# Output projection beside the attention: from full 128x128 matmuls in one stretch to 64x32 tiles in two parts

## The chip, the cores and the metric

The kernel runs on one core of a Trainium2 chip, as one launch. The metric is the device time of that launch in microseconds (us), the median of several runs.

## The reference

Two graph layers work on `x` of 8 batches x 2048 nodes x 256 features, in fp32, with one 2048 x 2048 0/1 adjacency for all batches. The first layer is multi-head attention (4 heads of 64) in which each query row takes a softmax over every chunk of 256 keys by itself, and the chunks' results are added up. The second is a graph attention of rank one. Cut to what matters here:

```python
h = jnp.maximum(_layernorm(x), 0.0)
q, k, v = (h @ Wq.T + bq), (h @ Wk.T + bk), (h @ Wv.T + bv)      # split into 4 heads of 64
scores = jnp.einsum('bhnd,bhjcd->bhnjc', q, kc) / 8.0              # 8 chunks j of 256 keys
scores = jnp.where(mask == 0, -10.0, jnp.clip(scores, -10.0, 10.0))
ctx = jnp.einsum('bhnjc,bhjcd->bhnd', jax.nn.softmax(scores, axis=-1), vc)
out = ctx @ Wo.T + bo + h                                          # the output projection
x = x + _layernorm(out) * gamma + beta
...                                                                # layer 1: rank-one graph attention
```

The change concerns `ctx @ Wo.T`, a product of 2048 x 256 by 256 x 256 for each batch.

## The kernel before, in words

The order of the instructions on every engine is written out by hand, and each engine runs its own queue in that order; waits between engines are put in by the framework from the data that they share.

A batch's attention has 32 steps: 4 blocks `nb` of 512 queries, times 8 chunks `j` of 256 keys. The loop in `gnn_two_layers` runs over `f`, and each `f` has two halves, `Attention.begin(f)` and `Attention.end(f)`. Several steps are in flight: `f-1` makes logits, `f-2` and `f-3` are multiplied with the values.

All attention matmuls are small tiles of TensorE: 64 rows (half of the contraction rows) by 32 columns, so eight of them fit at once, four in each half of the rows. "Half 0" below is rows 0 to 63, "half 1" is rows 64 to 127. The kernel always issues four matmuls for one half and then four for the other, so that both halves work side by side. An fp32 matmul appears in the trace as two weight loads and two matmul records.

- `logits(n, o, kt)` (L401): the logits of head `ORDER[o]`, into a PSUM tile `ps_s`, of which there are two. Heads 0 and 2 of the order use half 1, heads 1 and 3 use half 0.
- `clip(n, o)` (L441): VectorE reads the finished `ps_s` tile, clips and masks it into `e`, and so frees that tile.
- `values(n, half, c, kt)` (L417): products of `e` with the values, into two `ps_n` tiles. `sums(n, half)` (L429): the softmax denominators, into a `ps_t` tile, of which there are two; `invert` (L461) on ScalarE reads that. `scale` (L471) multiplies the two, and `gather` (L476) adds the result into `ctxT` by an accumulating DMA.
- `fence(before, after)` (L373): an empty instruction on SyncE that waits for some matmuls and lets others go. It stands where both halves of the rows write one bank of PSUM one after the other.

`begin(f)` issues on TensorE: `values(f-3)`, then pieces marked `pe`, then `logits(f-1, 1)` and `logits(f-1, 2)` in turn. `end(f)` issues: `values(f-2)`, `logits(f-1, 3, 0)`, `sums(f-2, 1)`, `logits(f-1, 3, 1)`, `logits(f, 0, 0)`, pieces, `sums(f-2, 0)`, `logits(f, 0, 1)`. On VectorE `begin` has clip 0 and the two scales, and `end` has `first` pieces, clip 1, clip 2, other pieces, clip 3.

The work that follows the attention of a block of queries is cut into pieces (`Between`) and laid beside the attention of the next block: `beside()` gives each piece a slot, counted in halves of `f`. Even slots fall into a `begin`, odd ones into an `end`; pieces without a mark in an even slot run in the `end` that follows, after clip 2. Three of the four blocks of a batch are treated so, 24 in all. The fourth block of each batch has its projection after the attention, by the unchanged `output` and `take`.

In the kernel before, slot 8 has `output(0)` and `output(1)` (L600): 8 matmuls of 128 x 128 x 256, 16 records, into both `ps_t` tiles. Slot 9 has `take` (L609), in which VectorE adds the residual `hn0` to 512 columns of PSUM at a time, and the layernorm's `stats` (L260, L261); the first two stand ahead of clip 1.

Of the kernel before, what the change touches and what calls it, by code (L numbers as in the profile page):

```python
# [8 lines left out]
F32 = mybir.dt.float32  # L9
# [4 lines left out]
ALU = mybir.AluOpType  # L14
# [3 lines left out]
P = 128  # L18
# [10 lines left out]
def gnn_two_layers(  # L29
# [18 lines left out]
    nc = tc.nc  # L48
    B, N, F = x.shape
    FC = F // P  # L50
    DH = F // HEADS
    Q = P // 4
# [3 lines left out]
    TB = NB // P  # L56
    NNB = N // NB
# [16 lines left out]
    def ps_t():  # L74
        return ps.tile([P, 512], F32, tag="t", name="ps_t")
# [4 lines left out]
    def ps_m():  # L80
        if turn_about[0]:
            turn_about[1] += 1
            if turn_about[1] % 2:
                return ps_n()
        return ps_t()
# [8 lines left out]
    work = ctx.enter_context(tc.tile_pool(name="work", bufs=2, reuse_waits="tile"))  # L94
# [14 lines left out]
    woT = const.tile([P, FC, F], F32, name="woT")  # L109
# [47 lines left out]
    def first(piece):  # L157

        piece.kind = "first"
        return piece  # L160

    def pe(piece):

        piece.kind = "pe"
        return piece


# [27 lines left out]
    def load_rows(t, half):  # L195
        rows = xpool.tile([P, HALF], I32, tag="x", name="rows", bufs=NNB)
        nc.sync.dma_start(rows, adj[t * P:(t + 1) * P, half * HALF:(half + 1) * HALF])
        return rows
# [32 lines left out]
    def adjacency(parts):  # L231


        def load(i):
            rows[i] = load_rows(*parts[i])

        def find(i):
            found[i] = missing_of(rows.pop(i), *parts[i])

        def turn(i):  # L240
            found[i] = turn_missing(found[i])

        def keep(i):
            keep_bounds(found.pop(i), *parts[i])

        finds = [9, 11, 15, 17, 21, 23, 29, 31]
        turns = [12, 12, 18, 18, 26, 26, 32, 32]
        todo = {}
        for i, (f, t) in enumerate(zip(finds, turns)):
            todo.setdefault(f - 6, []).append(lambda i=i: load(i))  # L250
            todo.setdefault(f, []).append(lambda i=i: find(i))
            todo.setdefault(t, []).append(pe(lambda i=i: turn(i)))
            todo.setdefault(t + 1, []).append(first(lambda i=i: keep(i)))
        return todo
# [18 lines left out]
    def norm_tiles(tag, bufs):  # L273
        mv = small.tile([P, TB, 2], F32, tag="mv", name="mv")
        rn = small.tile([P, 2, TB], F32, tag=tag, name=tag, bufs=bufs)
        return mv, rn
# [19 lines left out]
    class Projection:  # L296
# [32 lines left out]
        def take(self, nb, c):  # L329
            if c == 0:  # L330
                nc.vector.tensor_copy(self.hT[nb][:, 0, :], self.pt.pop(c))
            else:
                nc.scalar.activation(self.hT[nb][:, 1, :], self.pt.pop(c), AF.Copy)
# [37 lines left out]
    def fence(before, after):  # L371

        nop = nc.sync.nop()  # L373
        for x in before:
            tc.add_manual_dep(nop.ins, x.ins.name, SYNC, reason="both write one bank of PSUM")
        for x in after:
            tc.add_manual_dep(x.ins, nop.ins.name, SYNC, reason="both write one bank of PSUM")


    class Attention:  # L380
# [159 lines left out]
        def end(self, f, pieces=()):  # L540
            self.run(pieces, "first")
            if self.has(f - 1):
                self.clip(f - 1, 1)
                self.clip(f - 1, 2)
            self.run(self.rest, None)
            if self.has(f - 1):
                self.exponentials(f - 1, 1)
                self.exponentials(f - 1, 2)
            if self.has(f - 2):
                made = {}  # L550
                for kt in range(KT):
                    for half, c in ((0, 1), (1, 0)):
                        made.setdefault(c, []).extend(self.values(f - 2, half, c, kt))
                for c in range(2):
                    self.before[f - 2, c] = made[c]
            if self.has(f - 1):
                self.logits(f - 1, 3, 0)
            if self.has(f - 2):
                sums = self.sums(f - 2, 1)
            if self.has(f - 1):  # L560
                self.logits(f - 1, 3, 1)
            if self.has(f):
                self.logits(f, 0, 0)
            self.run(pieces, None)
            self.run(pieces, "pe")
            if self.has(f - 2):
                fence(sums, self.sums(f - 2, 0))
            if self.has(f):
                self.logits(f, 0, 1)
            if self.has(f - 1):  # L570
                self.clip(f - 1, 3)
                self.add(f - 1, 0)
# [8 lines left out]
    class Between:  # L581
# [12 lines left out]
        def output(self, t2):  # L594
            ctxT = self.attention.ctxT[self.nb]
            pp = self.pp[t2] = ps_m()
            for i in range(2):
                t = 2 * t2 + i
                for c in range(FC):
                    nc.tensor.matmul(  # L600
                        pp[:, i * F:(i + 1) * F], ctxT[:, c, t * P:(t + 1) * P], woT[:, c, :],
                        start=c == 0, stop=c == FC - 1,
                    )

        def take(self, t2):
            if t2 == 0:
# [90 lines left out]
        def beside(self):  # L697

            todo = {
                -3: [self.load],  # L700
                3: [lambda: self.residual(0)],
                4: [lambda: self.residual(1)],
                5: [lambda: self.bias(0)],
                6: [lambda: self.bias(1)],
                8: [pe(lambda: self.output(0)), pe(lambda: self.output(1)), lambda: self.beta(0)],
                9: [
                    first(lambda: self.take(0)), first(lambda: self.stats([0])),
                    first(lambda: self.take(1)), first(lambda: self.stats([1])), lambda: self.stats([2]),
                ],
                10: [lambda: self.stats([3]), lambda: self.beta(1)],  # L710
                12: [self.power],
                13: [self.shift],
                14: [lambda: self.scaled(range(TB))],
                15: [lambda: self.gamma(0)],
                16: [lambda: self.gamma(1)],
                18: [lambda: self.add(0)],
                20: [lambda: self.add(1)],
            }

            def at(n, *pieces):  # L720
                todo.setdefault(n, []).extend(pieces)

            if self.nb == NNB - 2:
                return todo
            for t, n in enumerate((20, 22, 26, 28)):
                at(n, lambda t=t: self.stats1([t]))
            at(29, self.power1)
            at(30, self.shift1)
            if self.nb == 1:
                at(31, lambda: self.norm1(0))  # L730
                at(32, lambda: self.norm1(1))
            return todo
# [115 lines left out]
    rows = {i: load_rows(*nearest[i]) for i in range(4)}  # L848
# [69 lines left out]
    def layer1_vector(i):  # L918
# [11 lines left out]
        1: [lambda: raws.update(o=load_output_weight(wo)), layer1_weight],  # L930
        2: [lambda: store_bounds(0), lambda: store_bounds(1)],
        5: [pe(lambda: turn_weight(raws["o"], woT))],
        6: [lambda: layer1_vector(0)],
        7: [lambda: layer1_vector(1)],
# [8 lines left out]
    for b in range(B):  # L943
# [3 lines left out]
        zero, low, mid, last = blocks  # L947
# [260 lines left out]
```

The softmax here doesn't subtract the row's maximum and nothing guards it: scores larger than these inputs give would overflow.

## Time and profile before

| what | value |
|---|---|
| device time, median of 3 runs | 3649.71 us (3645.97 to 3652.3) |
| profiled span | 3645.0 us |
| TensorE busy | 3607.6 us, 99% of the span |
| VectorE, ScalarE, GpSimd busy | 71%, 54%, 49% |
| granted TensorE clock | 0.999 |
| L600, the output projection | 512 matmul records, of which 448 into `ps_t` and 64 into `ps_n` |
| L609, its take by VectorE | 64 instructions, median 692 ns |
| L441, the clips | 1024 instructions, 1220 ns each |

"Busy" counts the time in which at least one record of the engine is open. Eight tiles of TensorE can be open at once, so the durations of the attention matmuls (590 ns each) don't add up to time; how fast the groups of four follow each other does. The view called windows gives the busy time of each engine in stretches of the span, and the timeline lists the groups of instructions by their start.

### The profile page before, as it was taken

The page shows a single profiled execution, that of the slowest core. Times are in us where ns is not written, and L with a number is a line of the kernel's source. Part 1 is how long each engine was busy: PE and PEld are TensorE (multiplying, and loading weights), DVE is VectorE, ACT ScalarE, POOL GpSimd, SP SyncE. Part 2 cuts the span into 40 slices and gives each one's busy share as a digit, 9 for nine tenths or more (in the row PEclk, how much of TensorE's full clock was granted, in tenths as well). Part 3 has the DMA queues.
Part 4 walks back from the last instruction along what each step waited for, and adds up shares of the span by engine and source line. Part 5 has one row for each costly group of instructions (what it writes and reads, how often), then busy time and mean ns, then how long its engine had stood idle before and what let it go on. Part 6 is the DMA issues. An engine that isn't in the chain of part 4 may idle for free.

```text
span 3645.0 us, 99457 instructions
## 1 busy us (share of the span) xinstructions
PE 3607.6 (99%) x43952; PEld 2210.2 (61%) x43952; DVE 2582.9 (71%) x3915; ACT 1958.0 (54%) x2975; POOL 1788.8 (49%) x1142
## 2 busy tenths in 40 slices
PE   7999999999999999999999999999999999999999
PEld 4444785547754577455874558645586455865568
DVE  5887577866777666776667866678576785767866
ACT  5677416774167732677326762367713667147650
POOL 0678016870178702786027850378403774048731
PEclk9999999999999999999999999999999999999999
DMA  7444113341133411343113431134312332124321
GB/s 224 115 104 97 44 53 83 83 106 29 64 81 82 103 34 59 83 95 88 47 47 83 101 77 47 53 83 95 77 52 59 86 87 64 47 53 89 77 53 35
DMA packets 133281, 276.93 MB, mean 76 GB/s; under 512 B 26608, under 2 KB 91888, under 8 KB 124656
## 3 DMA queue, kind: packets, MB, share of 16 engines
q0 software_dynamic: 32256, 117.45, 17.7%
q1 hardware_dynamic: 83952, 151.01, 12.1%
q8 instruction: 344, 5.64, 0.7%
q10 hardware_dynamic: 16640, 2.10, 0.4%
q14 instruction: 89, 0.73, 0.1%
HBM read 132.12 MB, written 20.97 MB: 42 GB/s over the span
## 4 chain that ended last, share of the span: by engine, by line
PE 95%; DMA 2%; ACT 1%; DVE 1%; POOL 0%; issue 0%; POOLq 0%; ACTq 0%; SPq 0%; DVEq 0%
PE ps_n L417 24%; PE ps_s L401 24%; PE ps_s L800 12%; PE ps_t L429 6%; PE ps_n L800 6%; PE ps_t L800 6%; PE ps_t L600 3%; PE ps_t L345 2%; PE ps_n L345 2%; PE ps_s L345 2%; PE ps_n L674 2%; PE ps_t L674 2%; PE ps_t L359 1%; PE ps_n L359 1%; DMA ctxT<-prod 1%; PE ps_t L292 1%
## 5 line engine op out<-in xcount | busy, mean ns | idle before, releaser
L456 POOL TENSOR_TENSOR both<-e 128x1024 f32<-128x1024 f32 x512 | 1218.2, 2409 | 660.3 <-PE ps_s L401 258.9
L441 DVE SCALAR_TENSOR_TENSOR e<-ps_s,bound 128x1024 f32<-128x1024 f32 x1024 | 1220.1, 1220 | 377.3 <-PE ps_s L401 375.3
L401 PE MATMUL ps_s<-q,k 64*32 64x512 f32 x16384 | 1362.6, 590 | 2.1 <-DVE e L441 2.1
L450 ACT ACTIVATE e<-e 128x1024 f32<-128x1024 f32 x1024 | 1049.2, 1049 | 549.8 <-DVE e L441 530.4
L417 PE MATMUL ps_n<-e,v 64*32 64x512 f32 x16384 | 1164.3, 590 | 6.3 <-DVE prod L471 4.0
L417 PEld LDWEIGHTS ps_n<-e,v 64*32 64x32 f32 x16384 | 446.2, 107 | 504.4 <-issue 393.3
L401 PEld LDWEIGHTS ps_s<-q,k 64*32 64x32 f32 x16384 | 435.7, 106 | 461.0 <-issue 332.4
L817 POOL TENSOR_TENSOR x<-x,r 128x256 f32<-128x256 f32 x128 | 98.5, 770 | 1137.5 <-DVE rz L810 1006.3
L429 PE MATMUL ps_t<-both,ones 64*32 64x512 f32 x4096 | 538.0, 591 | 0.5
L800 PE MATMUL ps_s<-g,w 128*128 128x257 f32 x2048 | 448.7, 380 | 0.0
L471 DVE TENSOR_TENSOR prod<-ps_n,rz 128x512 f32<-128x512 f32 x448 | 288.7, 686 | 192.4 <-PE ps_n L417 86.1
L800 PEld LDWEIGHTS ps_s<-g,w 128*128 128x128 f32 x2048 | 388.3, 190 | 54.9
L783 DVE SCALAR_TENSOR_TENSOR w<-bound,w 128x1024 f32<-128x1024 int8 x256 | 313.7, 1225 | 8.7
L800 PE MATMUL ps_n<-g,w 128*128 128x257 f32 x1024 | 292.6, 382 | 0.0
L800 PE MATMUL ps_t<-g,w 128*128 128x257 f32 x1024 | 290.1, 380 | 0.0
L777 DVE TENSOR_SCALAR w<-src,cd 128x512 f32<-128x512 f32 x512 | 265.2, 560 | 9.8 <-ACT src L771 9.4
L461 ACT ACTIVATE rz<-ps_t 128x512 f32<-128x512 f32 x256 | 152.6, 596 | 177.4 <-PE ps_t L429 102.6
L476 POOL DMA_DIRECT2D ctxT<-prod x224 | 194.5, 868 | 55.0 <-DVE prod L471 52.4
L800 PEld LDWEIGHTS ps_n<-g,w 128*128 128x128 f32 x1024 | 192.6, 190 | 43.4 <-issue 17.6
L800 PEld LDWEIGHTS ps_t<-g,w 128*128 128x128 f32 x1024 | 194.0, 189 | 28.1
L429 PEld LDWEIGHTS ps_t<-both,ones 64*32 64x32 f32 x4096 | 121.9, 106 | 93.0 <-SPq L373 52.3
L462 ACT ACTIVATE rz<-rz 128x512 f32<-128x512 f32 x256 | 161.4, 630 | 8.1
(127 smaller groups left out, 2849.4 us busy)
## 6 DMA issues: line engine op xcount, KB each, us to landing
ctxT<-prod POOLq DMA_DIRECT2D x224, 512.0 KB, 4.9
bound<-bound_d SPq DMA_DIRECT2D x62, 1024.0 KB, 5.3
xp<-in_x_dram SPq DMA_DIRECT2D x60, 512.0 KB, 4.7
rows<-in_adj_dram SPq DMA_DIRECT2D x32, 512.0 KB, 5.5
x<-in_x_dram SPq DMA_DIRECT2D x32, 512.0 KB, 5.3
out_dram<-x SPq DMA_DIRECT2D x31, 512.0 KB, 2.9
bound_d<-bound_part ACTq DMA_DIRECT2D x16, 128.0 KB, 4.5
bound_d<-bound SPq DMA_DIRECT2D x2, 1024.0 KB, 6.4
```

What stands on the lines that cost most here:

```text
L345: nc.tensor.matmul(pp, w[:, di, do * P:(do + 1) * P], self.hT[nb][:, di, :], start=di == 0, stop=di == FC - 1,)
L401: nc.tensor.matmul(self.s[n, o][c * Q:(c + 1) * Q, kt, :], self.k[p][rows, at:at + Q], self.q[p][rows, nb * NB:(nb + 1) * NB], start=True, ...
L417: made.append(nc.tensor.matmul(self.num[n, c][h * Q:(h + 1) * Q, :], self.v[rows, j * KT + kt, at:at + Q], self.e[n, p][rows, i * KT + kt, :],
L429: nc.tensor.matmul(self.total[n][h * Q:(h + 1) * Q, :], ones[rows, :], self.both[n, h // 2][rows, h % 2, :], start=half == 1, stop=half == 0,)
L441: nc.vector.scalar_tensor_tensor(self.e[n, p][:, i * KT:(i + 1) * KT, :], self.s.pop((n, o)), -CLIP * SC, bounds[nb][:, j * KT:(j + 1) * K ...
L450: nc.scalar.activation(e, e, AF.Exp, scale=1.0 / SC)
L456: nc.gpsimd.tensor_tensor(self.both[n, p], e[:, 0], e[:, 1], op=ALU.add)
L471: nc.vector.tensor_tensor(dst[:, c, :], self.num.pop((n, c)), self.rz[n], op=ALU.mult)
L476: nc.gpsimd.dma_start(self.ctxT[nb], self.prod.pop(n), accum_op=ALU.add)
L777: nc.vector.tensor_scalar(w[:, i, :], self.src[nb], self.cd[:, 0, j:j + 1], self.cd[:, 1, j:j + 1], op0=ALU.mult, op1=ALU.max,)
L783: nc.vector.scalar_tensor_tensor(two, bounds1[nb][:, j - 1:j + 1, :], 0.0, two, op0=ALU.is_gt, op1=ALU.mult)
L800: nc.tensor.matmul(accs[t][:, 0:F + 1], w[:, i, t * P:(t + 1) * P], g[:, j, :], start=j == 0, stop=j == NT - 1,)
```

## The change

The projection beside the attention is made in the same 64x32 tiles as the attention, so that TensorE need not change its tiling for it. Every matmul of 128 x 128 x 256 becomes eight of 64 x 32 x 256. Half 0 and half 1 of the contraction rows both contribute to every output and may not write one bank of PSUM together, so the work is cut into two parts ("turns"): in turn 0 half 0 writes `pp[0]` and half 1 writes `pp[1]`, in turn 1 they change places. Turn 0 stands where the projection stood, ahead of the two slots of logits of `begin`; turn 1 follows them, at the head of the TensorE work of `end`; and a fence between the turns sees that a bank's first writers are done. Slot 9's `take` becomes four additions of 256 columns (`take_tiles`), which stand between clip 1 and clip 2 on VectorE, and the `stats` move to later places.

```diff
         def end(self, f, pieces=()):
...
                 self.clip(f - 1, 1)
+            self.run(pieces, "pe1")
+            self.run(pieces, "mid")
+            if self.has(f - 1):
                 self.clip(f - 1, 2)
...
+        def output_tiled(self, turn):
+            ctxT = self.attention.ctxT[self.nb]
+            if turn == 0:
+                self.pp = {t2: ps_t() for t2 in range(2)}
+                self.made = {}
+            made = {}
+            for i in range(2):
+                for c in range(FC):
+                    for half in range(2):
+                        t2 = half ^ turn
+                        rows = slice(half * DH, (half + 1) * DH)
+                        for h in range(4):
+                            at = (2 * t2 + i) * P + h * Q
+                            job = nc.tensor.matmul(
+                                self.pp[t2][h * Q:(h + 1) * Q, i * F:(i + 1) * F], ctxT[rows, c, at:at + Q],
+                                woT[rows, c, :], start=turn == 0 and i == 0 and c == 0,
+                                stop=turn == 1 and i == 1 and c == FC - 1,
+                            )
+                            made.setdefault(t2, []).append(job)
+            for t2 in range(2) if turn else ():
+                fence(self.made[t2], made[t2])
+            self.made = made
+
+        def take_tiles(self, i):
...
+            for t2 in range(2):
+                nc.vector.tensor_tensor(
+                    self.o4[:, 2 * t2 + i, :], self.pp[t2][:, i * F:(i + 1) * F], self.hn0[t2][:, i, :], op=ALU.add
+                )
...
-                8: [pe(lambda: self.output(0)), pe(lambda: self.output(1)), lambda: self.beta(0)],
+                8: [pe(lambda: self.output_tiled(0)), lambda: self.stats([0]), lambda: self.beta(0)],
                 9: [
-                    first(lambda: self.take(0)), first(lambda: self.stats([0])),
-                    first(lambda: self.take(1)), first(lambda: self.stats([1])), lambda: self.stats([2]),
+                    pe1(lambda: self.output_tiled(1)), mid_clips(lambda: self.take_tiles(0)),
+                    mid_clips(lambda: self.take_tiles(1)), lambda: self.stats([1]),
                 ],
-                10: [lambda: self.stats([3]), lambda: self.beta(1)],
+                10: [lambda: self.stats([2]), lambda: self.beta(1)],
+                11: [lambda: self.stats([3])],
```

## The prediction

> **What bounds the kernel now.** I read the page's busy shares and its chain of waits first, then the windows over four steps of `f`, then the timeline around one projection.
>
> ```profile
> PE 3607.6 (99%) x43952; PEld 2210.2 (61%) x43952; DVE 2582.9 (71%) x3915; ACT 1958.0 (54%) x2975; POOL 1788.8 (49%) x1142
> ...
> PE 95%; DMA 2%; ACT 1%; DVE 1%; POOL 0%; issue 0%; POOLq 0%; ACTq 0%; SPq 0%; DVEq 0%
> ```
>
> TensorE is busy throughout and is 95% of the chain, so time is won only by taking TensorE time away, and lost by making TensorE wait. The windows are, in order: a plain step, the step with a projection, and the two steps after it.
>
> ```profile
> 597.11:604.83 7.73, 7.73 (x152) 4.02 (x144) 6.06 (x6) 5.24 (x7) 5.53 (x4) 1.00 0.37 70
> 624.57:636.62 12.04, 12.04 (x172) 6.25 (x164) 9.07 (x15) 5.24 (x6) 6.82 (x4) 1.00 0.24 46
> 636.62:644.34 7.72, 7.72 (x152) 3.88 (x144) 6.52 (x9) 5.24 (x6) 6.87 (x4) 1.00 0.19 37
> 644.34:652.15 7.81, 7.81 (x148) 3.63 (x140) 5.96 (x7) 5.83 (x9) 5.78 (x4) 1.00 0.65 141
> ```
>
> A plain step is 7.72 us. It has 144 small matmul records, 18 groups of four for each half of the rows, so a group takes 0.429 us per half: TensorE runs without a gap although VectorE is busy for about 6 of the 7.7 us. The step with the projection is 4.32 us longer, and a busy share of 100% hides that not all of this is work.
>
> ```profile
> 624.57 0.61 PE L417 MATMUL ps_n<-e,v 64*32 64x512 f32 x4
> 624.68 0.61 PE L401 MATMUL ps_s<-q,k 64*32 64x512 f32 x4
> 625.00 2.00 PE L417 MATMUL ps_n<-e,v 64*32 64x512 f32 x28
> 626.93 3.72 PE L600 MATMUL ps_t<-woT,ctxT 128*128 128x256 f32 x16
> 630.58 1.95 PE L401 MATMUL ps_s<-q,k 64*32 64x512 f32 x32
> 632.32 1.92 PE L417 MATMUL ps_n<-e,v 64*32 64x512 f32 x32
> ...
> 629.03 0.69 DVE L609 TENSOR_TENSOR o<-ps_t,hn 128x512 f32<-128x512 f32 x1 [1.15 <-PE ps_t L600]
> 630.76 0.69 DVE L609 TENSOR_TENSOR o<-ps_t,hn 128x512 f32<-128x512 f32 x1 [0.35 <-PE ps_t L600]
> 632.57 2.36 DVE L441 SCALAR_TENSOR_TENSOR e<-ps_s,bound 128x1024 f32<-128x1024 f32 x2 [0.57 <-PE ps_s L401]
> ```
>
> The reader is to see that at 624.57 half 0 already starts the values while half 1, at 624.68, still has a last group of logits: half 1 is 0.54 us behind. Half 0 has done its four groups by 624.57 + 1.71 = 626.29, half 1 by 626.82; L600 starts at 626.93. So half 1 loses 0.11 us and half 0 0.64. After 3.65 us both halves start level at 630.58.
>
> **What the Trainium skill says.** "TensorEngine Tiling (Array Packing)", Key Properties: a change of the tiling mode drains TensorE. The trace agrees: 0.11 us for the later half, 0.64 for the earlier. "TensorE: Matmul & The Clock Gate", Part 3, The mechanism: matmuls are in strict program order at start and end. The trace differs: half 0's values start ahead of half 1's logits, which precede them in the program. The measurement decides, and the slip between the halves matters below. "PSUM — Partial Sum Buffer", on bank collisions: different row tiles may not access one bank together; software must synchronize. That is what the fence is for; no run here shows a collision. Price: "TensorEngine Tiling", Instruction Overhead, puts some 60 cycles on each matmul, an estimate of 25 ns at the 2.4 GHz that the TensorE page gives.
>
> **The change part by part.**
>
> *Removed.* L600 in 24 places; 16 records at 0.216 us are 3.45 us of work each. What a place costs in all: after the first and second block of a batch the halves are 0.54 us apart again two steps later (half 0 at 652.15 as at 624.57), because in the window from 644.34 half 1 waits for the second scale, which waits for a DMA. So three steps, 12.04 + 7.72 + 7.81 = 27.57, less 3 x 7.72 = 23.16, give 4.41 us. After the third block no such step comes before the batch's next full-size matmuls, which align the halves anyway; there half 1, which finishes last, lost 4.32 - 0.43 (its lag falls from 0.54 to 0.11) = 3.89 us.
>
> *Added on TensorE.* 64 matmuls of 256 columns are 128 records, 16 groups of four per half. At half of 0.429 us a group this is 16 x 0.215 = 3.44 us, the same work as before; the trace shows no small matmul of 256 columns. Bounds: 3.44 if the array sets the pace; 6.86 if a 256-column record costs as much as one of 512 (weight load included). I take 3.44: eight records now have 215 ns, 27 ns each, over the 25 ns that the price gives at full clock, and a small weight load of 107 ns fits into 215. No tiling changes and no alignment: 0.97 us saved at the first two blocks, 0.45 at the third.
>
> *The fence.* Half 0's turn 1 waits for half 1's turn 0. Two slots of logits, 4 groups or 1.71 us, lie between; half 0 is 0.54 ahead, so about 1.0 us is left after the last record's 0.16 us tail. SyncE's fence at L373 shows no wait of TensorE itself, only of weight loads (52.3 us in 248). Behind it are the values; cost nothing. The `ps_t` tile that half 1 needs at once was freed by the Ln of `invert`, which ends at 625.51 against 626.82; nothing either.
>
> *VectorE, the new wait.* `take_tiles` waits for the whole of turn 1 (only its first instruction waits for TensorE), and clip 2 is queued behind it. Who waits for clip 2: `logits(f, 0)` in half 1, which needs its `ps_s` tile. Costs: two scales of 0.68 take 1.29 together, so 512 columns are 0.61 apart; clips of 1.22 take 2.36, so 1024 are 1.14 apart; hence 256 columns are 0.61 - 0.27 = 0.34. From the moment T at which half 1 ends turn 1: 0.28 (tail 0.16 and 0.11 to start, as from L600's end at 630.65 to 630.76), takes 4 x 0.34 = 1.36, clip 2 1.14 and 0.08 to its end, 0.08 to TensorE: T + 2.94. Half 1 meanwhile has values 1.71 and sums 0.86: T + 2.57. It waits 0.37. Then VectorE has stats 0 and 1, 2 x 0.64 (L260 to L261 0.46, L261 0.18), clip 3 1.14, clip 0 1.22, then 0.08: from T + 2.78 to T + 6.50. Half 1 needs clip 0 for `logits(f, 2)` after four groups of logits and four of values, 2.94 + 3.43 = T + 6.37. It waits 0.13 more. Together 0.5, with two reloads of weights 0.52 us per block. In the kernel before, takes and two stats lay under L600 and the logits, ending at 632.00 before clip 1 could start at 632.57: hidden. Now the takes are not. Clip 1 itself comes earlier and waits for nothing new; stats 2 and 3 in the next step fit its free VectorE time (6.5 of 7.7 busy). SyncE, GpSimd and ScalarE keep their order.
>
> *Sum.* Some 15 blocks win 0.97 - 0.52 = 0.45, some 9 (the third of each batch, and the first of batch 0, which starts with the halves nearly level) lose 0.52 - 0.45 = 0.07: 6.75 - 0.63 = 6.1 us. 3649.7 - 6.1 = 3643.6 us. With the waits at 0.35 to 0.75 the gain is 10 to 1 us.
>
> **The rivals.**
> A, the wait on clip 2 is hidden: if the takes start by parts, or half 1's lag absorbs them, 0.1 us per block is left: 15 x 0.87 + 9 x 0.35 = 16, 3634 us. For it: plain steps absorb all of VectorE's lateness. Against: takes wait for half 1's end, so a lag of half 1 shifts both alike.
> B, small 256-column matmuls do not reach the array's pace. At worst 3.42 us x 24 = 82 - 6: 3726 us; half of it, 3685. For it: twice the records per time, never shown. Against: after stalls, groups of eight start 7 ns apart.
> C, the waits chain: VectorE's or the fence's lateness costs 1.1 us per block, as when stats push clip 3 and the next scales: 9 x 0.65 + 15 x 0.13 = 8 slower, 3657 us. For it: VectorE's queue from the takes to clip 0 is 6.2 us without a gap. Against: everything after it has slack of half a microsecond or more.
>
> **How the numbers follow.** Forecast 0.48, A 0.28, B 0.10, C 0.14. 0.2% is 7.3 us. The forecast's 10 to 1 us of gain gives faster 0.14, same 0.33, slower 0.01; A faster 0.26, same 0.02; B slower 0.10; C same 0.06, slower 0.08: faster 0.40, same 0.41, slower 0.19. The range leaves out B and the far ends of A and C: 3632 to 3662.
>
> **What would show it.** Right: small records of L633 in groups of four 0.215 us apart per half, no gap ahead of them, the halves still 0.5 us apart after them; the four takes in a row 0.3 us after turn 1's end; a gap of about 0.4 us in half 1 before `logits(f, 0)`, released by the clip, and a step with projection of about 11.7 us. Wrong: groups further apart than 0.215 (B), TensorE waiting on SyncE at L633 or for scales (C), or no gap at `logits(f, 0)` (A).

## The result and the profile after

The changed kernel takes 3634.21 us (median of 4 runs, 3632.24 to 3639.86) against 3648.95 for the kernel before in the same comparison: a ratio of 0.9962, interval 0.9945 to 0.9979, so 7.7 to 20 us less. The profiled span is 3630.0 us against 3645.0. The prediction had 3643.6 us, a gain of 6.1.

The busy times and the shares of the chain of waits, on the page of the changed kernel:

```profile
PE 3594.1 (99%) x46640; PEld 2205.1 (61%) x46640; DVE 2577.4 (71%) x3963; ACT 1961.8 (54%) x2975; POOL 1791.5 (49%) x1142
...
PE 97%; DMA 1%; ACT 1%; DVE 1%; issue 0%; POOL 0%; ACTq 0%; POOLq 0%; SPq 0%; DVEq 0%
```

TensorE is the bound as before, with 2688 more records (24 blocks of 128 in place of 16). Its busy time fell by 13.5 us although the arithmetic is the same: "busy" counts a time as work even when one half of the rows stands still in it. Where that was is seen in the same block as in the prediction. First the windows: the step with the projection and the two steps after it (columns: length, then PE, PEld, DVE, ACT, POOL, clock, DMA share, GB/s).

```profile
621.44:632.69 11.25, 11.25 (x280) 6.71 (x272) 7.75 (x14) 5.04 (x6) 6.86 (x4) 1.00 0.26 50
632.69:640.71 8.02, 8.02 (x156) 3.16 (x148) 7.76 (x12) 5.45 (x7) 6.85 (x4) 1.00 0.23 44
640.71:648.43 7.72, 7.72 (x152) 4.01 (x144) 5.86 (x7) 5.85 (x9) 5.78 (x4) 1.00 0.56 129
```

The step is 11.25 us, where it was 12.04. The next one is 0.30 longer than a plain step, and the third is a plain 7.72, where it was 7.81. In sum, 11.25 + 8.02 - 2 x 7.72 - 3.44 of work leaves 0.39 us lost per block; before it was 0.97, the third step included.

The timeline of TensorE through the projection (start, length, instructions; L425 is the values, L409 the logits, L437 the sums, L633 the projection):

```profile
621.44 0.61 PE L425 MATMUL ps_n<-e,v 64*32 64x512 f32 x4
621.54 0.61 PE L409 MATMUL ps_s<-q,k 64*32 64x512 f32 x4
...
623.16 0.40 PE L633 MATMUL ps_t<-woT,ctxT 64*32 64x256 f32 x4
623.26 0.61 PE L425 MATMUL ps_n<-e,v 64*32 64x512 f32 x4
623.37 1.79 PE L633 MATMUL ps_t<-woT,ctxT 64*32 64x256 f32 x52
624.88 0.62 PE L409 MATMUL ps_s<-q,k 64*32 64x512 f32 x4
624.98 0.61 PE L633 MATMUL ps_t<-woT,ctxT 64*32 64x256 f32 x8
...
626.60 0.41 PE L633 MATMUL ps_t<-woT,ctxT 64*32 64x256 f32 x4
626.70 0.61 PE L409 MATMUL ps_s<-q,k 64*32 64x512 f32 x4
626.82 1.79 PE L633 MATMUL ps_t<-woT,ctxT 64*32 64x256 f32 x52
628.33 0.63 PE L425 MATMUL ps_n<-e,v 64*32 64x512 f32 x4
628.43 0.61 PE L633 MATMUL ps_t<-woT,ctxT 64*32 64x256 f32 x8
...
631.00 0.61 PE L437 MATMUL ps_t<-both,ones 64*32 64x512 f32 x4
631.33 1.08 PE L409 MATMUL ps_s<-q,k 64*32 64x512 f32 x8
```

Half 0 starts turn 0 at 623.16 while half 1 still has a group of values, and is done with the 8 groups of this turn at 624.88, when its logits start: 1.72 us, 0.215 per group, the work and nothing more. Half 1 is still 0.54 behind after both turns: half 0 starts its values at 628.33, and half 1 has two more groups of the projection from 628.43 on, until about 628.865. Turn 1 starts at 626.60, right behind half 0's logits, so the fence holds nobody. The price appears at the end: half 1's last group of sums starts at 631.00, so it could go on at 631.43, but its logits do not start then. The weight loads show it, and VectorE's timeline shows why:

```profile
631.78 0.13 PEld L409 LDWEIGHTS ps_s<-q,k 64*32 64x32 f32 x5 [0.73 <-DVE e L449]
```

```profile
626.85 1.23 DVE L449 SCALAR_TENSOR_TENSOR e<-ps_s,bound 128x1024 f32<-128x1024 f32 x1 [2.10 <-PE ps_s L409]
629.18 1.42 DVE L648 TENSOR_TENSOR o<-ps_t,hn 128x256 f32<-128x256 f32 x4 [1.10 <-PE ps_t L633]
630.51 1.22 DVE L449 SCALAR_TENSOR_TENSOR e<-ps_s,bound 128x1024 f32<-128x1024 f32 x1
631.64 0.42 DVE L268 BATCH_NORM_STATS2 stats<-o 128x6 f32<-128x256 f32 x1
...
632.19 0.40 DVE L268 BATCH_NORM_STATS2 stats<-o 128x6 f32<-128x256 f32 x1
...
632.72 2.32 DVE L449 SCALAR_TENSOR_TENSOR e<-ps_s,bound 128x1024 f32<-128x1024 f32 x2
```

VectorE is idle from 628.08 to 629.18, waiting for turn 1. Then it makes the four takes (L648), and clip 2 (630.51 to 631.73) behind them frees the tile that half 1 needs: a wait of 0.37 us, from 631.43 to about 631.80.

### The profile page after: what moved, and what is told of

The parts are those of the page before. It is cut to its first block, busy times and chain, and to the rows that moved or that the text cites. A ratio compares the mean times of both kernels' runs of the same rounds, so it can differ in the third digit from the quotient of the medians.

```text
span 3630.0 us, 104929 instructions
## 1 busy us (share of the span) xinstructions
PE 3594.1 (99%) x46640; PEld 2205.1 (61%) x46640; DVE 2577.4 (71%) x3963; ACT 1961.8 (54%) x2975; POOL 1791.5 (49%) x1142
## 4 chain that ended last, share of the span: by engine, by line
PE 97%; DMA 1%; ACT 1%; DVE 1%; issue 0%; POOL 0%; ACTq 0%; POOLq 0%; SPq 0%; DVEq 0%
PE ps_s L409 24%; PE ps_n L425 24%; PE ps_s L848 12%; PE ps_t L437 6%; PE ps_n L848 6%; PE ps_t L848 6%; PE ps_t L633 2%; PE ps_t L353 2%; PE ps_n L353 2%; PE ps_s L353 2%; PE ps_t L721 2%; PE ps_n L721 2%; PE ps_t L367 1%; PE ps_n L367 1%; PE ps_t L300 1%; PE ps_n L300 1%
## 5 line engine op out<-in xcount | busy, mean ns | idle before, releaser
L409 PE MATMUL ps_s<-q,k 64*32 64x512 f32 x16384 | 1434.1, 590 | 2.1 <-DVE e L449 2.1
L425 PE MATMUL ps_n<-e,v 64*32 64x512 f32 x16384 | 1220.5, 590 | 4.8 <-ACT e L458 2.3
L425 PEld LDWEIGHTS ps_n<-e,v 64*32 64x32 f32 x16384 | 451.9, 107 | 482.1 <-issue 391.9
L409 PEld LDWEIGHTS ps_s<-q,k 64*32 64x32 f32 x16384 | 451.9, 106 | 468.2 <-issue 325.4
L437 PE MATMUL ps_t<-both,ones 64*32 64x512 f32 x4096 | 539.0, 591 | 0.6
L437 PEld LDWEIGHTS ps_t<-both,ones 64*32 64x32 f32 x4096 | 115.2, 106 | 92.7 <-SPq L381 47.0
```

The source lines that it names most:

```text
L409: nc.tensor.matmul(self.s[n, o][c * Q:(c + 1) * Q, kt, :], self.k[p][rows, at:at + Q], self.q[p][rows, nb * NB:(nb + 1) * NB], start=True, ...
L425: made.append(nc.tensor.matmul(self.num[n, c][h * Q:(h + 1) * Q, :], self.v[rows, j * KT + kt, at:at + Q], self.e[n, p][rows, i * KT + kt, :],
L437: nc.tensor.matmul(self.total[n][h * Q:(h + 1) * Q, :], ones[rows, :], self.both[n, h // 2][rows, h % 2, :], start=half == 1, stop=half == 0,)
```

## The experiments

Two theories were to be told apart. The first is the prediction's: the place of the projection costs more than its drain because it takes away the lead of half 0 (0.54 us), and the changed kernel pays for keeping it with a wait for clip 2. The rival: takes and fence are hidden, and the gain is simply the change of tiling that is no longer made. Each kernel was run five times unless another number stands beside it; ratios are to runs of the kernel before in the same comparison. Edits are against the changed kernel unless said otherwise.

**Takes behind clip 2 (e1, and again as e8).** The four takes change places with clip 2 on VectorE, nothing else.

```diff
-            self.run(pieces, "mid")
             if self.has(f - 1):
                 self.clip(f - 1, 2)
+            self.run(pieces, "mid")
```

> The changed kernel with clip 2 ahead of the takes on VectorE. Theory (half 1 waits 0.37 us per block for clip 2, which stands behind the takes): the wait is gone, 24 x 0.39 = 9.4 us less than the changed kernel, 3625 us; the trace shows half 1 of logits(f, 0) right behind sums without a gap, and the step with the projection at 11.2 us. Rival (what the changed kernel won does not depend on the takes; the wait only makes up for a lead that the halves have anyway): within 2 us of the changed kernel.

Measured: 3628.86 us, ratio 0.9943 [0.993, 0.9955]. The same step and its successor, and VectorE around the takes:

```profile
625.86:637.03 11.17, 11.17 (x280) 7.05 (x272) 8.37 (x15) 5.24 (x6) 6.87 (x4) 1.00 0.26 50
637.03:644.75 7.72, 7.72 (x152) 4.05 (x144) 7.10 (x11) 5.24 (x6) 6.87 (x4) 1.00 0.19 37
```

```profile
631.26 2.36 DVE L449 SCALAR_TENSOR_TENSOR e<-ps_s,bound 128x1024 f32<-128x1024 f32 x2 [2.10 <-PE ps_s L409]
633.53 1.41 DVE L648 TENSOR_TENSOR o<-ps_t,hn 128x256 f32<-128x256 f32 x4
```

Clips 1 and 2 run in one piece and the takes follow without idle time: 11.17 + 7.72 - 15.44 - 3.44 = 0.01 us lost per block. So the wait for clip 2 is real, is on TensorE's path, and is what the order of takes and clip 2 makes it. The ratio fell by less than the 9 us that 24 waits come to: the 3625 us of the theory were not reached, and the rival's 2 us were passed. The same kernel once more:

> Clip 2 ahead of the four takes once more, for its distance from the changed kernel. Theory (0.37 us per block less than the changed kernel, 9 us, of which the first run's median showed 3 because of chance in the start and in single DMA waits): 17 to 18 us less than the kernel before at the blocks of the trace, and a start that differs from the first run's. Rival (the order of the takes costs elsewhere what it saves at the blocks): the same later start and the same smaller saving as in the first run.

Measured: 3627.04 us, 0.9944 [0.9931, 0.9958]. The repetition gives the same ratio as e1, so the smaller saving was not chance in the first run. By the ratios this is the faster version: both are below the changed kernel's 0.9962 and, measured again beside e1 (e4), 0.9955 [0.9943, 0.9968].

> The changed kernel itself once more, for its ratio to the kernel before from more rounds and for a second trace. Theory (each block wins 0.58 us at the first two of a batch and 0.06 at the third, 10 us in all; the rest of the 15 us between the two profiles is chance in the start and in single DMA waits): the same savings at the blocks in the second trace, and other ones elsewhere; ratio 0.9965 to 0.997. Rival (the rest belongs to the change): 15 us again, 0.9959, at the same places.

e4 took 3631.78 us. The ratios of the two orders are 0.0011 to 0.0019 apart, 4 to 7 us, though the intervals overlap: that the wait is gone is shown by the traces, how much of it the whole kernel gains is not settled by the times. e4 also went against its own theory: the ratio is below the expected 0.9965 to 0.997, and its trace gains 15 us again, in the same places (the table below).

**Two takes of 512 columns in place of four of 256 (e2).**

```diff
-                    ... mid_clips(lambda: self.take_tiles(0)),
-                    mid_clips(lambda: self.take_tiles(1)), ...
+                    ... mid_clips(lambda: self.take(0)),
+                    mid_clips(lambda: self.take(1)), ...
```

> The changed kernel with two takes of 512 columns in the place of four of 256. Theory (the chain on VectorE from turn 1 to clip 2 sets the wait): 2 x 0.61 in the place of 4 x 0.335 us shortens the wait by 0.12 us, 2.9 us over 24 blocks, 3631 us. Rival (the wait is set by the end of turn 1 alone, or is hidden): no change, 3634 us.

Measured: 3632.03 us, 0.9954 [0.9941, 0.9966]. In the trace each block is 0.13 us shorter at its place, 3.1 us in all, as it should be if the takes' length is on the path; the ratios (e4 0.9955) cannot tell 3 us.

**Two takes, behind clip 2 (e7).** Both edits together. If the takes' length matters only through clip 2, it has no effect here.

> Clip 2 ahead of the takes, and two takes of 512 columns in the place of four of 256. Theory (with clip 2 ahead nothing waits for the takes any more): as with four takes after clip 2, 3629 us, and no wait of TensorE for a take or for clip 2 at the blocks; 0.66 us less per block than the kernel before where half 0 keeps its lead. Rival (the takes still hold up the sums, which need the PSUM tile that they read): 0.12 us less per block than with four, 3 us.

Measured: 3627.55 us, 0.9945 [0.9933, 0.9958], the same as e1 and e8. Behind clip 2 the takes are hidden.

**Stats ahead of clip 2 (e6).** One pair of stats moves from behind clip 2 to between the takes and clip 2: a longer wait of a known size.

```diff
-                8: [pe(lambda: self.output_tiled(0)), lambda: self.stats([0]), lambda: self.beta(0)],
+                8: [pe(lambda: self.output_tiled(0)), lambda: self.beta(0)],
...
+                    mid_clips(lambda: self.stats([0])), lambda: self.stats([1]),
```

> The changed kernel with the first stats of each block (0.54 us of VectorE) between the takes and clip 2. Theory (half 1 waits for clip 2, and the wait grows by all that stands ahead of it on VectorE): 24 x 0.54 = 13 us more than the changed kernel, 3645 us, with a wait of 0.9 us in half 1 ahead of logits(f, 0). Rival (the halves' lead or the free time of VectorE takes it up): within 3 us of the changed kernel.

Measured: 3648.02 us (13 runs), 0.9998 [0.999, 1.0006]: all that the change had won is gone. TensorE's timeline in its step:

```profile
635.74 0.61 PE L437 MATMUL ps_t<-both,ones 64*32 64x512 f32 x4
636.07 0.63 PE L409 MATMUL ps_s<-q,k 64*32 64x512 f32 x4
637.04 0.63 PE L409 MATMUL ps_s<-q,k 64*32 64x512 f32 x4 [0.35 <-DVE e L449]
637.07 0.63 PE L437 MATMUL ps_t<-both,ones 64*32 64x512 f32 x4
```

Half 1 is due at 635.74 + 0.43 = 636.17 and goes on at 637.04: the wait has grown from 0.37 to 0.87, by 0.50, close to the 0.54 of the stats. Half 0's sums (637.07), issued behind the waiting logits, are held too: due at 636.50, they lose 0.57. The bracket on the line gives the idle gap of TensorE as a whole, 0.35 us.

**The tiling alone, in one stretch (e3).** Both turns stand where the projection stood, and the takes stand ahead of clip 1 again. The tiling change is gone, the two slots between the turns are gone as well.

```diff
-                8: [pe(lambda: self.output_tiled(0)), ...
+                8: [pe(lambda: self.output_tiled(0)), pe(lambda: self.output_tiled(1)), ...
                 9: [
-                    pe1(lambda: self.output_tiled(1)), mid_clips(lambda: self.take_tiles(0)),
-                    mid_clips(lambda: self.take_tiles(1)), lambda: self.stats([1]),
+                    first(lambda: self.take_tiles(0)), first(lambda: self.take_tiles(1)), lambda: self.stats([1]),
```

> The changed kernel with both turns in slot 8, ahead of the logits, and the takes ahead of clip 1 as before the change. Theory (the two slots of logits between the turns hide the fence and keep half 0 ahead): half 0 waits for half 1's turn 0 and for SyncE, about 0.36 us after half 1's end, so its lead of 0.54 us is lost at every block and bought back at the first two of a batch; the wait for clip 2 is gone, because the takes lie under the logits: about 3641 us. Rival (the split is of no use, the fence is short): the wait for clip 2 is gone and nothing comes in its place, 3625 us.

Measured: 3649.0 us (13 runs), 0.9999 [0.9991, 1.0008]: a miss by 8 us, and no gain whatever. TensorE, its weight loads, and the sum of these waits (us, times, longest) from the view of the waits:

```profile
626.49 0.40 PE L633 MATMUL ps_t<-woT,ctxT 64*32 64x256 f32 x4
626.60 0.61 PE L425 MATMUL ps_n<-e,v 64*32 64x512 f32 x4
626.71 4.31 PE L633 MATMUL ps_t<-woT,ctxT 64*32 64x256 f32 x124
630.80 1.07 PE L409 MATMUL ps_s<-q,k 64*32 64x512 f32 x16
```

```profile
629.05 1.48 PEld L633 LDWEIGHTS ps_t<-woT,ctxT 64*32 64x32 f32 x64 [0.60 <-SPq L381]
```

```profile
PEld ps_t L633 <- SPq L381: 14.4, 24, 0.6
```

Half 1 starts its last group of values at 626.60 and so ends turn 0 at 626.60 + 0.43 + 1.72 = 628.75. Turn 1 waits for SyncE, whose fence needs that end. I had expected half 0 alone to lose its lead and half 1 to go straight on; but no weights are loaded for either half until 629.05, so half 1 is held for 0.30 us as well (its own fence needs only half 0's turn 0, which was done at 626.49 + 1.72 = 628.21; that it stands behind half 0's wait, which precedes it in the program, is inferred from this). At 630.80 the logits start level. 24 times 0.30 is 7 of the 8 us that the expectation missed. From half 0's first group of the projection (626.49) to its logits this is 4.31 us, as long as with the full-size matmuls (626.29 to 630.58, 4.29). So the removal of the tiling change wins nothing by itself; a fence without work between its two sides costs the same, and it costs it in the same two places, as the table below shows.

**A full-size matmul put back (e5, against e1).** One 128 x 128 x 8 matmul before turn 0; turn 0 overwrites what it writes.

```diff
+                nc.tensor.matmul(self.pp[0][:, 0:8], ident_b, ident_b[:, 0:8], start=True, stop=True)
```

> The kernel with clip 2 ahead of the takes, and one full-size bf16 matmul of 128 x 128 x 8 ahead of turn 0, whose result turn 0 overwrites: the halves are brought level at every block, and the tiling changes twice, while the projection itself stays in small tiles. Theory (most of the cost of the full-size projection was the lost lead of half 0, bought back two steps later in the first two blocks of a batch): 0.11 us for the drain, some 0.3 for the small matmul and the way back, and 0.53 again at the first two blocks; 24 x 0.4 + 16 x 0.53 = 18 us more than without it, nearly back at the kernel before. Rival (a change of tiling costs the drain alone): 24 x 0.4 = 10 us more, and no new wait two steps later.

Measured: 3647.13 us (13 runs), 0.9995 [0.9986, 1.0003], 18 us above e1 (19 by the ratios), for 24 matmuls:

```profile
622.49 0.61 PE L425 MATMUL ps_n<-e,v 64*32 64x512 f32 x4
622.60 0.61 PE L409 MATMUL ps_s<-q,k 64*32 64x512 f32 x4
622.92 2.00 PE L425 MATMUL ps_n<-e,v 64*32 64x512 f32 x28
624.86 0.18 PE L624 MATMUL ps_t<-ident_b 128*128 128x8 bf16 x1
624.96 1.96 PE L634 MATMUL ps_t<-woT,ctxT 64*32 64x256 f32 x64
...
631.87 0.61 PE L409 MATMUL ps_s<-q,k 64*32 64x512 f32 x4
632.17 0.63 PE L437 MATMUL ps_t<-both,ones 64*32 64x512 f32 x4
```

Half 0 ends its values at 622.49 + 1.72 = 624.21 and half 1 at 622.60 + 0.43 + 1.72 = 624.75. The full-size matmul starts 0.11 later, and 0.10 after that both halves start level. The half that is behind loses 0.21 us; half 0 loses 0.75. 24 x 0.21 is only 5 us. Most of the rest is the lead, which half 1 gives back in two pieces. With the halves level, its sums are due at 631.87, when half 0's logits start, but they start at 632.17: by the program they need the `ps_t` tile that the takes, now last on VectorE, still read (the trace names no releaser there). That is 0.30 us at every block, 7 us in all, and it comes from a wait that the expectation did not have. Two steps later half 1 falls back by the rest, 4.4 us over the first two blocks of the batches, where 8.5 were expected. So the expected 18 us came out in total, but not with the expected split, and partly by luck. The rival's 10 us do not reach the 18, and the new wait two steps later that it excluded is there. With e3, which loses the same without any change of tiling, this separates the theories.

**Where the time of each trace went.** Worked out from the traces, in us against the kernel before; one trace per kernel. The clock is half 1, the half that ends last: the start of the last matmul of every run of values. "At the block" is the step with the projection and the next one, over all 24 blocks. "Later" is the third step, for the first two blocks of each batch (16) and for the third (8).

```
                       start   at the block   later, 1 and 2   later, 3   elsewhere   sum
changed kernel         -1.67      -1.99          -8.75          -1.25      -1.28    -14.94
again (e4)             -1.96      -1.99          -8.85          -1.34      -1.26    -15.41
takes last (e1)        +2.70     -10.64          -7.63          -0.61      +1.00    -15.16
takes last (e8)        -2.57     -10.63          -8.48          -1.04      -0.09    -22.81
two takes (e2)         +0.36      -5.08          -8.84          -1.29      +1.21    -13.63
two, last (e7)         +4.13     -10.85          -7.41          -0.68      -0.99    -15.79
one stretch (e3)       +0.03      -0.18          +0.40          +2.43      -3.36     -0.68
full tile (e5)         -1.92      +2.82          -3.23          +1.54      +1.85     +1.06
stats ahead (e6)       +1.61     +10.66          -8.45          -1.34      +2.81     +5.30
```

The middle columns repeat to 0.1 us where a kernel was run twice as it was (e4), and to 0.9 between e1 and e8. The start, which is the same code in all of them, differs by 6.7 us between traces: a single span can be off by that much, so the columns tell more than the sums. For half 1 most of the changed kernel's gain is "later", two steps behind the place that was edited. Half 0 has it at the block: its values start 0.49 us earlier two steps on (19.27 us instead of 19.76), and 0.09 more in the third step. It is one saving of 0.58 us, seen from either half.

## Why the prediction was right, and where it was off

The measured 3634.21 us lie in the stated range, but the size was right in part by luck. The gain of 14 us by the ratio is more than twice the forecast 6.1 and above its 10 to 1 us, though the interval (7.7 to 20) reaches into that; the range held it because rival A, the hidden wait, had been let in, and A turned out false. What was right is most of the mechanism, term by term:

*The cost of the old place: right, but for the third blocks.* Of the 0.97 us per place, 0.54 was to be the lead that half 1 gives back two steps later. That is the column "later, 1 and 2": in 15 of the 16 blocks half 1 saves 0.16 to 1.07 us there, with a median of 0.53 and a mean of 0.58. The first block of batch 0, which starts with the halves nearly level, has nothing to lose (0.00), as the prediction said. For the third blocks it had put this at nothing; in batches 3, 6 and 7 half 1 waited there too, 0.35 to 0.40 us that the changed kernel saves. e5 brings part of the loss back by levelling the halves, e3 all of it. That the halves fall apart again because half 1 waits for a scale behind a DMA is read from one block of the kernel before,

```profile
647.03 1.29 DVE L471 TENSOR_TENSOR prod<-ps_n,rz 128x512 f32<-128x512 f32 x2 [0.94 <-DMA ctxT<-prod]
```

where the scales wait 0.94 us for the DMA that still reads `prod`. In the changed kernel the scales of that step wait for nothing:

```profile
642.80 1.29 DVE L479 TENSOR_TENSOR prod<-ps_n,rz 128x512 f32<-128x512 f32 x2
```

In e1 they still wait 0.29 us for the DMA (647.12), and yet the step takes a plain 7.72 us: half 1, which is 0.54 behind, needs them later. A second `prod` tile, which would take this wait away by itself, was not tried, so that the DMA is the cause is argued, not shown.

*The pace of the small matmuls: right.* 0.215 us per group was taken for 256 columns, and 0.215 is measured. That is 27 ns per record with both halves at work, over the 25 that the prediction had estimated from the Trainium skill's "TensorEngine Tiling (Array Packing)", Instruction Overhead. Rival B falls: a record with its weight load takes no longer than half of one of 512 columns.

*The fence: right.* Among the waits of the changed kernel, the only ones of L633's weight loads are for their issue; SyncE is not there.

```profile
PEld ps_t L633 <- issue: 19.2, 96, 0.2
```

That the two slots of logits hide the fence is shown by e3, where they are gone and SyncE is waited for 24 times.

*The wait for clip 2: right to 0.01 us.* With half 1 leaving turn 1 at about 628.865 the prediction's sum puts the restart at 631.80, and it waits 0.37; e1 takes the wait away, e6 lengthens it as worked out. The sign "a step with projection of about 11.7 us" did not come, since the wait is half 1's alone: half 0 starts its next values 0.09 us late (11.25), and the other 0.30 stand in the step after (8.02). Rival A gave 3634 us, which the kernel reached, but not for its reason: the wait is there, and without it (e1) the blocks give 18.3 us (10.64 + 7.63) where the changed kernel has 10.7.

*The second wait, for clip 0: wrong.* The prediction has VectorE at "stats 0 and 1, 2 x 0.64", which makes clip 0 late by 0.13. The pair of stats are chained: the second starts at 632.19, beside the tail of the first pair, so they are 0.54 apart (631.64, 632.19, 632.72). The two clips end at 632.72 + 2.32 = 635.04, before half 1 needs clip 0 at 631.80 + 3.43 = 635.23. The cost of a block is 0.39 us, not 0.52: 24 x 0.13 = 3.1 us. The length of a pair of stats had been taken for its distance to the next, though the prediction had kept the two apart for clips and scales.

*The sum: too small.* With 0.39, the prediction's own terms are 15 x (0.97 - 0.39) + 9 x (0.45 - 0.39) = 9.2 us, where it had 6.1; the trace has 1.99 + 8.75 = 10.7 at these places, and 1.25 more behind the third blocks. The ratios say 14 (0.9962) and 16 (e4, 0.9955). What is left in the two traces is the start (1.7 and 2.0), which varies by more than that from trace to trace, and 1.3 "elsewhere", which is the same in both; where that comes from stays open. In e1 and e8 the "later" columns and "elsewhere" give back 2 to 4 us of the 8.6 that the exchange saves at the blocks, as e8's rival had it in part; why stays open too. Without the start, e1 and e8 are 4.4 to 7 us ahead of the changed kernel's two traces, as the ratios have it (4 to 7).

*The rivals.* Rival C, chained waits, falls for this kernel: the second step after the projection is a plain 7.72. e6 shows how little was missing: one pair of stats ahead of clip 2 takes the whole gain away.

## What to carry to other kernels

Where small tiles work in two halves of the rows, the lead of one half over the other is worth something: whatever brings them level (a change of tiling, or a fence with no work between its two sides) costs the lead, here 0.54 us against a drain of 0.11, and may be paid for two steps later. In the queue of the engine behind, put first what frees a buffer that the bounding engine will ask for next, and what nobody waits for last; here the exchange of two neighbours takes away a wait of 0.37 us per block. Before a change is credited to its idea, do its parts one at a time: the tiling without the split won nothing.

## What the runs showed of the hardware

- The two halves of the rows run out of program order by 0.54 us, in L633 as in the attention. The Trainium skill, "TensorE: Matmul & The Clock Gate", Part 3, The mechanism, has matmuls in strict order at their start and end; the traces differ, for 64 x 32 tiles in different rows.
- Yet a matmul of one half that waits for another engine can hold the other half: half 1 stood for 0.30 us at half 0's wait for SyncE (e3), and half 0's sums for 0.57 behind half 1's logits, which precede them in the program (e6).
- A change to a full-size tile and back took 0.11 and 0.10 us for the later half, the small matmul included in the second (e5, 8 columns in bf16); half 0 stood for 0.75. "TensorEngine Tiling (Array Packing)", Key Properties, names the drain without a figure.
- Additions of 256 columns from PSUM follow each other at about 0.335 us though each lasts 0.416: four take 1.42.
